# A two-layer graph network kernel: projection biases added in PSUM by VectorE, and the places of five pieces in a written-out order

## The chip, the cores and the metric

The kernel runs on 1 core of one Trainium2 chip. The time is device microseconds from launch to end; a smaller time is better. The engines go by the names of the profile: PE (TensorE, with PEld for its weight loads), DVE (VectorE), ACT (ScalarE), POOL (GpSimd) and SP (SyncE, which here only issues DMAs). PSUM is the memory that PE writes; everything else on the core lies in SBUF.

## The reference

There are 128 graphs (B) of 128 nodes (N) with 64 features (F). About one entry in eight of an adjacency matrix is not zero.

```python
# layer 0: an edge network
h    = maximum(layernorm(x), 0)
mask = (adj > 0)
a    = h @ W1a                                   # W1 = [W1a; W1b], H = 192
e    = relu(a[:, :, None] + (h[:, :, None] - h[:, None]) @ W1b + b1)
hm   = einsum('bjkh,bjk->bjh', e, mask)          # sum over the neighbours k of j
x    = x + hm @ W2 + mask.sum(-1)[..., None] * b2
# layer 1: plain aggregation
h    = maximum(layernorm(x), 0)
x    = x + (adj @ h) @ W.T
```

## The kernel before

Graphs are taken four at a time (G = 4), so there are 32 groups. The inner value of the edge network splits into a part of node j, with the bias, and a part of node k. The kernel doesn't build all 128 x 128 pairs. It gathers each node's neighbours with one-hot matrices: the nodes are cut into four quarters (q), in each quarter a neighbour of j gets a slot (six slots, D = 6), and the few edges that fit no slot go through an extra list of up to 128 edges.

**Jobs.** A group is 24 jobs. A job fills one of three PSUM buffers `g` of two banks with matmuls (tiles S3, k3 and id3) and drains it. Jobs of kind 0 (16 of the 24) are drained by a reduction on DVE into `hm`; jobs of kind 1 (jobs 4, 5, 10, 11, 16, 17, 22, 23, counted from 0) by a Relu on ACT into `T`, which POOL then sums. The same three buffers also take the projection `pp`, twice a group; a second pool of two one-bank buffers takes all smaller products.

**Pieces between the jobs.** After job t the pieces that three tables list for t are issued. `AHEAD` prepares group g+1: `pre_adj` (t = 0; transposes adj into `adjT`, makes `maskT`), `pre_norm`, `pre_hT`, `pre_rank` (3; ranks `qs`), `pre_slots` (3, 4, 6; one-hot `S`, and then twelve DMAs that make S3), `pre_count` (5; `dn`, `ns`, `half`, `nb`), `pre_proj` (7 and 12), `pre_stack` (12; twelve DMAs from `ca` to k3), and `pre_edge_a`, `pre_edge_b`, `pre_place`, `pre_edge_c`, `pre_edge_d` (9 to 23; tiles `et`, `R`, `qj`, `RT`, `S2`). `OWN` makes the edge list's values X (14 and 15, PSUM tile `px`). `BEHIND` ends group g-1: `slot_sum` and `edge_sum` (0, 1; PSUM tile `pe`, result `u`), `edge_sum1`, `post0` (product with W2, PSUM tile `py`, copied by ACT to `ys`), `post1` (transposes back, adds the residual, statistics), `post2` (the second normalization, `h`), `post3` (the aggregation with adjT, `pga`, copied by ACT to `agg`) and `post4` (the last product `po`, the residual and the store of `ot`).

**The projection.** `pre_proj(g, r)` multiplies hT of two graphs with the 448 columns of `wp` into `pp`: 192 columns for node k, 192 for node j and 64 for the output. The bias belongs to the last 256 columns. It is added by PE: a matmul of a tile of ones with `biasp`, whose rows hold the bias split into three bf16 parts (built once in `weights_c`). ACT then copies the first 384 columns as bf16 (`ca`, part 0), makes z and e from pp, DVE subtracts to get `rest`, ACT makes part 1 of ca from it, and POOL part 2. The three parts together carry the fp32 value.

**What sets the order.** PE's instructions stand in the program's order. In the main loop those of the other engines are placed by the framework's scheduler, which also chooses which PSUM buffer a tile gets; within an engine they then run strictly in that order. The framework also adds the waits.

Of the kernel before, what the change touches and what calls it, by code (L numbers as in the profile page):

```python
# [8 lines left out]
F32 = mybir.dt.float32  # L9
BF16 = mybir.dt.bfloat16  # L10
I32 = mybir.dt.int32
AF = mybir.ActivationFunctionType
ALU = mybir.AluOpType
# [137 lines left out]
def kernel(  # L151
# [28 lines left out]
    def mm(*args, **kw):  # L180
        return tc.keep_in_program_order(nc.tensor.matmul(*args, **kw))  # L181
# [21 lines left out]
    vec, act, pool, sp = (Engine(e) for e in (nc.vector, nc.scalar, nc.gpsimd, nc.sync))  # L203

    B, N, F = x.shape
    H = W1.shape[1]
    O = W2.shape[1]
    P = 128
# [19 lines left out]
    with ExitStack() as main:  # L228
        const = main.enter_context(tc.tile_pool(name="const", bufs=1))
        loads = main.enter_context(tc.tile_pool(name="loads", bufs=2))  # L230
        grp = main.enter_context(tc.tile_pool(name="grp", bufs=2))
        one = main.enter_context(tc.tile_pool(name="one", bufs=1))
# [4 lines left out]
        def gtile(name):  # L237
            return ps_g.tile([P, 2, 512], F32, tag="g", name=name)

        def mtile(name):  # L240
            return ps_m.tile([P, 512], F32, tag="m", name=name)
# [7 lines left out]
        w2bd = const.tile([P, 2, O], F32, tag="w2bd", name="w2bd")  # L249
# [3 lines left out]
        ident = const.tile([P, P], F32, tag="ident", name="ident")  # L253
        make_identity(nc, ident)

        id64 = const.tile([P, 4], F32, tag="id64", name="id64")
        vec.tensor_tensor(id64, ident[:, 0:4], ident[:, F : F + 4], ALU.add)
        ones = const.tile([P, P], F32, tag="ones", name="ones")
        pool.memset(ones, 1.0)
        oneb = const.tile([P, P], BF16, tag="oneb", name="oneb")  # L260
# [11 lines left out]
        for q in range(Q):  # L272
            s = slice(q * QN, (q + 1) * QN)
# [43 lines left out]
        bias = const.tile([P, H + O], F32, tag="bias", name="bias")  # L317
        wp = const.tile([P, 2 * H + O], F32, tag="wp", name="wp")
        wab = wp[:, H : 2 * H]
        biasp = const.tile([P, H + O], BF16, tag="biasp", name="biasp")  # L320

        def weight_loads():
            act.dma_start(w2a, W2[0:C0, :])
# [33 lines left out]
            return pc  # L357

        def weights_c(pc):
            left = bias  # L360
            for i in range(3):
                pt = one.tile([P, H + O], BF16, tag=f"bp{i}", name=f"bp{i}")
                vec.tensor_copy(pt, left)

                if i == 0:
                    vec.tensor_scalar(biasp, pt, id64[:, i : i + 1], None, ALU.mult)
                    vec.tensor_copy(wp[:, 2 * H : 2 * H + O], pc[:, 0:O])
                else:
                    vec.scalar_tensor_tensor(
                        biasp, pt, id64[:, i : i + 1], biasp, ALU.mult, ALU.add  # L370
                    )
                if i < 2:
                    nxt = one.tile([P, H + O], F32, tag=f"br{i}", name=f"br{i}")
                    vec.tensor_tensor(nxt, left, pt, ALU.subtract)
                    left = nxt

        def weights_d():
            pl = mtile("pl")
# [5 lines left out]
        def bc(t, n, axis):  # L384
            shape = list(t.shape)
            shape.insert(axis, n)
            return t.unsqueeze(axis).to_broadcast(shape)
# [150 lines left out]
        def pre_proj(g, r):  # L538

            d = groups[g]  # L540
            if r == 0:

                d["ca"] = grp.tile([P, 3, 2, G, H], BF16, tag="ca", name=f"ca{g}")

                d["z"] = grp.tile([P, G, C0], F32, tag="z", name=f"z{g}")
                d["z1"] = grp.tile([P, 2, 2, C1], F32, tag="z1", name=f"z1{g}")
                d["e"] = grp.tile([P, G, O], F32, tag="e", name=f"e{g}", bufs=3)
            pp = gtile(f"pp{g}_{r}")
            for p in range(2):
                s = slice(p * F, (p + 1) * F)  # L550
                mm(
                    pp[:, p, 0 : 2 * H + O], d["hT"][s, r], wp[s, :],
                    start=True, stop=False, skip_group_check=True,
                )
            for p in range(2):
                s = slice(p * F, (p + 1) * F)
                mm(
                    pp[:, p, H : 2 * H + O], oneb[s, :], biasp[s, :],
                    start=False, stop=True, skip_group_check=True,
                )  # L560
            x = pp[:, :, 0 : 2 * H].rearrange("n p (t u) -> n p t u", t=2)
            parts = [
                d["ca"][:, i].rearrange("n t (p r) u -> n r p t u", p=2)[:, r] for i in range(3)
            ]
            act.activation(parts[0], x, AF.Copy)
            rest = tmp.tile([P, 2, 2, H], F32, tag="rest", name=f"rest{g}_{r}")

            def zs():
                for p in range(2):
                    b = 2 * p + r  # L570
                    for to, us, f in (
                        (d["z"][:, b], slice(0, C0), AF.Abs),
                        (d["z1"][:, r, p], slice(C0, H), AF.Relu),
                    ):
                        act.activation(to, x[:, p, 1, us], f, scale=d["ns"][:, b : b + 1])


            def es():
                for p in range(2):
                    b = 2 * p + r  # L580
                    act.activation(
                        d["e"][:, b], pp[:, p, 2 * H : 2 * H + O], AF.Copy,
                        scale=d["dn"][:, 0, b : b + 1],
                    )

            def second():
                act.activation(parts[1], rest, AF.Copy)

            def third(engine):
                for t in range(2):  # L590
                    engine.tensor_tensor(
                        parts[2][:, :, t], rest[:, :, t], parts[1][:, :, t], ALU.subtract
                    )

            def add_x():
                pool.tensor_tensor(d["e"], d["e"], d["x"], ALU.add)

            if g == 0:
                vec.tensor_tensor(rest, x, parts[0], ALU.subtract)
                return zs, es, second, third, add_x  # L600
            zs()
            es()
            vec.tensor_tensor(rest, x, parts[0], ALU.subtract)
            second()
            third(pool)
            if r == 1:
                add_x()
# [143 lines left out]
        def post0(g):  # L751
            d = groups[g]
            py = mtile(f"py{g}")
            d["py"] = py
            for p in range(2):
                s = slice(p * O, (p + 1) * O)
                mm(
                    py[s, 0 : 2 * N], w2h,
                    d["u0"][:, 2 * p : 2 * p + 2].rearrange("h r j -> h (r j)"),
                    start=True, stop=False, skip_group_check=True,  # L760
                )
            w = w2bd.rearrange("h p o -> h (p o)")
            mm(
                py[:, 0 : 2 * N], w, d["u1"].rearrange("h r j -> h (r j)"),
                start=False, stop=True, skip_group_check=True,
            )
            d["ys"] = tmp.tile([P, 2, N], F32, tag="ys", name=f"ys{g}", bufs=1)
            act.activation(
                d["ys"].rearrange("p r j -> p (r j)"), py[:, 0 : 2 * N], AF.Copy
            )  # L770
# [47 lines left out]
        class Job:  # L818
# [71 lines left out]
        AHEAD = {  # L890
            0: (pre_adj,),
            2: (pre_norm, pre_hT,),
            3: (pre_rank, lambda g: pre_slots(g, 0, 2),),
            4: (lambda g: pre_slots(g, 2, 4),),
            5: (pre_count,),
            6: (lambda g: pre_slots(g, 4, D),),
            7: (lambda g: pre_proj(g, 0),),
            9: (pre_edge_a,),
# [10 lines left out]
        BEHIND = {  # L909
            0: (slot_sum,),  # L910
            1: (edge_sum,),
            4: (edge_sum1,),
            8: (post0,),
            10: (post1,),
            15: (post2,),
            16: (post3,),
            19: (post4,),
        }

        ORDER = []  # L920
# [6 lines left out]
        def pieces(table, t, g):  # L927
            if 0 <= g < NG:
                for f in table.get(t, ()):
                    if (f, g) not in early:  # L930
                        f(g)
# [21 lines left out]
        pc = weights_b()  # L953
# [30 lines left out]
        for g in range(NG):  # L984
            if 0 < g < NG - 1:
                load(g + 1)
            order = ORDER0 if g == 0 else ORDERL if g == NG - 1 else ORDER
            for t, args in enumerate(order):
                job = Job(g, *args)
                job.fill()  # L990
                job.drain()
                if g == 0 and t in FIRST:
                    FIRST[t](0)
                pieces(OWN, t, g)
                pieces(BEHIND, t, g - 1)
                pieces(AHEAD, t, g + 1)
        for t in range(T):
            pieces(BEHIND, t, NG - 1)
        om = one.tile([P, 1], F32, tag="om", name="om")
# [34 lines left out]
```

## Time and profile before

| | |
|---|---|
| time, median of 3 runs | 1000.9 us (998.99 to 1002.17) |
| profiled execution | 1005.13 us, span 1003.4 us |
| busy: PE, DVE, POOL, ACT | 94%, 80%, 76%, 70% of the span |
| TensorE clock granted, mean | 0.978 of full |
| distance from one maskT to the next | 29.9 us, mean of 29 in the steady part |
| bias matmuls of pp | 128, 18.1 us busy |
| DMAs for S3 and k3 | 372 and 384, all issued by SP |

A row of the page's groups gives line, engine, operation, tile written <- tiles read, shapes and count; then busy time, the mean of one in ns, and the engine's idle time just before, with what ended most of it. A row of the timeline gives start (us), duration, engine, instruction and count, and in brackets the idle time before it. Rows of equal instructions that follow each other are merged. The next instruction of an engine often starts before the duration shown has run out, so a queue's speed is read from start to start. Almost every line is L198 or L181, since a helper issues the instructions: the tile names tell them apart.

### The profile page before, as it was taken

The numbers are of one execution on the slowest core, as the hardware profiler recorded it, in microseconds if no ns is written. First come the engines' busy times: TensorE is split into PE (matmuls) and PEld (weight loads), VectorE is DVE, ScalarE is ACT, GpSimd is POOL, SyncE is SP. The second block draws the span as 40 slices with busy tenths as digits, with TensorE's granted clock in tenths as the row PEclk, the third lists the DMA queues.
The fourth block names the chain that finished last, engine by engine and source line by source line (L and its number), as shares of the span: only waits on it lengthen the run. The fifth ranks groups of instructions, "written<-read, shape, count | busy, mean of one in ns | idle before, by whom it ended". The sixth has DMA issues, their size and how long they took to land.

```text
span 1003.4 us, 26630 instructions
## 1 busy us (share of the span) xinstructions
PE 947.9 (94%) x9994; PEld 695.8 (69%) x9994; DVE 801.2 (80%) x1769; ACT 706.3 (70%) x1732; POOL 767.5 (76%) x1134
## 2 busy tenths in 40 slices
PE   3899999999999999999999999999999999999996
PEld 2577776677776777777677767677767777777674
DVE  7677888877888878788887787887888887788863
ACT  5557876667877767787677785677787677787652
POOL 3287877787877878877788786778877788787783
PEclk9599999999999999999999999999999999999997
DMA  3626665556766555766555765555766655665520
GB/s 87 134 69 160 153 139 131 127 121 150 157 138 139 129 122 136 164 143 142 126 125 126 159 148 123 124 126 136 164 141 138 134 127 124 157 148 127 111 60 13
DMA packets 88293, 129.89 MB, mean 129 GB/s; under 512 B 47200, under 2 KB 63968, under 8 KB 88160
## 3 DMA queue, kind: packets, MB, share of 16 engines
q1 hardware_dynamic: 87584, 127.98, 56.4%
q8 instruction: 80, 1.31, 0.5%
q14 instruction: 53, 0.43, 0.1%
q10 hardware_dynamic: 576, 0.16, 0.1%
HBM read 13.01 MB, written 4.19 MB: 17 GB/s over the span
## 4 chain that ended last, share of the span: by engine, by line
PE 37%; DVE 23%; ACT 19%; DMA 7%; POOL 6%; issue 4%; SPq 3%; DVEq 0%; POOLq 0%; ACTq 0%
PE g L181 21%; DVE hm L198 7%; DVE S L198 7%; PE pe L181 7%; DMA k<-ca 6%; ACT ca L198 5%; ACT et L198 4%; POOL T L198 4%; SPq L198 3%; ACT h L198 3%; ACT T L198 3%; DVE u L198 3%; POOL ca L198 2%; ACT z L198 2%; PE px L181 2%
## 5 line engine op out<-in xcount | busy, mean ns | idle before, releaser
L198 POOL TENSOR_TENSOR T<-T 128x192 f32<-128x192 f32 (+2 forms) x768 | 545.7, 717 | 124.3 <-ACT T L198 84.4
L198 DVE TENSOR_REDUCE hm<-g 128x64 f32<-128x768 f32 x512 | 473.4, 950 | 117.0 <-PE g L181 113.2
L181 PEld LDWEIGHTS <-k 96*128 96x128 bf16 (+1 forms) x6144 | 412.8, 104 | 213.9 <-issue 87.0
L181 PE MATMUL g<-S,k 96*128 96x384 bf16 (+1 forms) x2048 | 392.5, 333 | 34.9 <-DMA k<-ca 18.5
L181 PE MATMUL g<-id,k 96*128 96x192 bf16 (+1 forms) x4096 | 383.9, 248 | 0.0
L198 ACT ACTIVATE T<-g 128x768 f32<-128x768 f32 x256 | 210.2, 823 | 51.7 <-PE g L181 45.7
L198 POOL TENSOR_TENSOR ca<-rest,ca 128x384 bf16<-128x384 f32 x126 | 113.9, 924 | 85.3 <-ACT ca L198 83.6
L198 ACT ACTIVATE ca<-pp 128x768 bf16<-128x768 f32 x64 | 51.4, 804 | 63.7 <-PE pp L181 63.7
L198 DVE TENSOR_TENSOR S<-qs,rks 128x1024 bf16<-128x1024 bf16 x93 | 86.8, 934 | 0.0
L198 ACT ACTIVATE hT<-ph 128x256 f32<-128x256 f32 x32 | 12.3, 384 | 89.4 <-PE ph L184 89.4
L181 PE MATMUL pe<-RT,X 128*64 128x128 f32 (+1 forms) x512 | 71.3, 282 | 0.0
L181 PE MATMUL pp<-wp,hT 64*128 64x448 f32 x256 | 68.5, 613 | 0.0
L198 ACT ACTIVATE z<-pp,ns 128x128 f32<-128x128 f32 (+1 forms) x256 | 66.0, 348 | 0.0
L198 DVE TENSOR_TENSOR rest<-pp,ca 128x768 f32<-128x768 f32 x64 | 60.7, 949 | 3.0 <-ACT ca L198 2.8
L198 ACT ACTIVATE ca<-rest 128x768 bf16<-128x768 f32 x64 | 55.2, 862 | 9.3 <-DVE rest L198 9.2
L181 PEld LDWEIGHTS pe<-RT,X 128*64 128x64 f32 (+1 forms) x512 | 53.4, 166 | 5.3 <-issue 5.3
L198 ACT ACTIVATE et<-et,half 128x128 f32<-128x128 f32 x128 | 56.8, 449 | 0.0
L181 PE MATMUL px<-ca,S 128*128 128x192 bf16 x384 | 52.7, 246 | 0.0
L181 PE MATMUL px<-ca,R 128*128 128x192 bf16 x384 | 52.6, 246 | 0.0
L198 ACT ACTIVATE h<-x,mrb,rsb 128x64 f32<-128x64 f32 x128 | 51.6, 479 | 0.8 <-DVE mrb L198 0.8
L181 PE MATMUL pe<-ident,z 128*128 128x128 f32 x192 | 49.9, 287 | 0.0
L198 ACT ACTIVATE h<-x,mra,rsa 128x64 f32<-128x64 f32 x128 | 48.7, 432 | 1.1 <-DVE mra L198 1.1
(128 smaller groups left out, 1203.9 us busy)
## 6 DMA issues: line engine op xcount, KB each, us to landing
S<-S SPq DMA_DIRECT2D x372, 192.0 KB, 4.0
k<-ca SPq DMA_DIRECT2D x384, 96.0 KB, 2.2
adj<-in_adj_dram SPq DMA_DIRECT2D x32, 256.0 KB, 3.1
x<-in_x_dram SPq DMA_DIRECT2D x32, 128.0 KB, 2.7
out_dram<-ot SPq DMA_DIRECT2D x32, 128.0 KB, 2.2
w<-in_L_gnn_W_dram SPq DMA_DIRECT2D x2, 96.0 KB, 4.4
bias<-in_L_gnn_b_dram ACTq DMA_DIRECT2D x1, 96.0 KB, 3.8
w2a<-in_L_gnn_W_dram ACTq DMA_DIRECT2D x1, 32.0 KB, 2.1
```

Source lines behind the costliest of these rows:

```text
L181: return tc.keep_in_program_order(nc.tensor.matmul(*args, **kw))
L198: ins = f(*args, **kw)
```

## The change

Two things are changed. First, the bias of the projection: the two matmuls with `biasp` are gone, and so are `biasp`, `id64` and the eight DVE instructions in `weights_c` that built it (with the one for id64, nine in all). In their place one DVE `tensor_tensor` adds the fp32 bias in place to 256 columns of both halves of `pp` in PSUM, before ACT and DVE read it. Second, the places of BEHIND's pieces: edge_sum1 from 4 to 3, post0 from 8 to 9, post1 from 10 to 11, post3 from 16 to 21, post4 from 19 to 23; at t = 3, 9 and 21 the piece of AHEAD now comes before that of BEHIND. In post0 the product with u1 comes before those with u0.

```diff
         def weights_c(pc):
-            left = bias
-            for i in range(3):
...
+            vec.tensor_copy(wp[:, 2 * H : 2 * H + O], pc[:, 0:O])
...
                 mm(
                     pp[:, p, 0 : 2 * H + O], d["hT"][s, r], wp[s, :],
-                    start=True, stop=False, skip_group_check=True,
-                )
-            for p in range(2):
-                s = slice(p * F, (p + 1) * F)
-                mm(
-                    pp[:, p, H : 2 * H + O], oneb[s, :], biasp[s, :],
-                    start=False, stop=True, skip_group_check=True,
-                )
+                    start=True, stop=True, skip_group_check=True,
+                )
+            biased = pp[:, :, H : 2 * H + O]
+            vec.tensor_tensor(biased, biased, bc(bias, 2, 1), ALU.add)
...
         BEHIND = {
             0: (slot_sum,),
             1: (edge_sum,),
-            4: (edge_sum1,),
-            8: (post0,),
-            10: (post1,),
+            3: (edge_sum1,),
+            9: (post0,),
+            11: (post1,),
             15: (post2,),
-            16: (post3,),
-            19: (post4,),
+            21: (post3,),
+            23: (post4,),
         }
...
                 pieces(OWN, t, g)
+                if t in (3, 9, 21):
+                    pieces(AHEAD, t, g + 1)
                 pieces(BEHIND, t, g - 1)
-                pieces(AHEAD, t, g + 1)
+                if t not in (3, 9, 21):
+                    pieces(AHEAD, t, g + 1)
```

More of the change, by code (lines that the diff above doesn't have):

```diff
@@ L254 @@
         make_identity(nc, ident)
-        id64 = const.tile([P, 4], F32, tag="id64", name="id64")
-        vec.tensor_tensor(id64, ident[:, 0:4], ident[:, F : F + 4], ALU.add)
         ones = const.tile([P, P], F32, tag="ones", name="ones")
@@ L319 @@
         wab = wp[:, H : 2 * H]
-        biasp = const.tile([P, H + O], BF16, tag="biasp", name="biasp")
         def weight_loads():
@@ L359, in weights_c @@
         def weights_c(pc):
-            left = bias
-            for i in range(3):
[L362 to L370, printed above, removed]
-                    )
[L372 to L375, printed above, removed]
+            vec.tensor_copy(wp[:, 2 * H : 2 * H + O], pc[:, 0:O])
         def weights_d():
@@ L754, in post0 @@
             d["py"] = py
+            w = w2bd.rearrange("h p o -> h (p o)")
+            mm(
+                py[:, 0 : 2 * N], w, d["u1"].rearrange("h r j -> h (r j)"),
+                start=True, stop=False, skip_group_check=True,
+            )
             for p in range(2):
@@ L759, in post0 @@
                     d["u0"][:, 2 * p : 2 * p + 2].rearrange("h r j -> h (r j)"),
-                    start=True, stop=False, skip_group_check=True,
+                    start=False, stop=True, skip_group_check=True,
                 )
[L762 to L766, printed above, removed]
             d["ys"] = tmp.tile([P, 2, N], F32, tag="ys", name=f"ys{g}", bufs=1)
```

## The prediction

> **What bounds the kernel now.** I read the busy shares first, then who waits for whom, then one group of the steady part (391 to 425 us) engine by engine in order of time.
>
> ```profile
> PE 947.9 (94%) x9994; PEld 695.8 (69%) x9994; DVE 801.2 (80%) x1769; ACT 706.3 (70%) x1732; POOL 767.5 (76%) x1134
> ```
>
> ```profile
> PE g L181 <- DMA k<-ca: 18.5, 22, 7.2
> PE g L181 <- DVE hm L198: 15.2, 31, 0.6
> ```
>
> TensorE (PE) is hardly ever idle, and the waits in front of it are small: 0.5 us a group for VectorE (DVE), and some tenths, where a group begins, for the last DMA of k3. So PE has about 1 us a group to spare, and each other engine is free for 20 to 30% of the time. An average doesn't say where that time lies; the order of time does. A group repeats every 29.9 us (the 29 distances between maskT instructions, from 67.9 to 935.4 us). The stretch that the change touches, DVE first, then ScalarE (ACT), then PE:
>
> ```profile
> 395.02 0.68 DVE L198 TENSOR_SCALAR maskT<-adjT 128x512 bf16<-128x512 f32 x1 [1.13 <-PE pe L181]
> ...
> 401.37 2.80 DVE L198 TENSOR_REDUCE hm<-g 128x64 f32<-128x768 f32 x3
> 404.09 0.95 DVE L198 TENSOR_TENSOR rest<-pp,ca 128x768 f32<-128x768 f32 x1
> ...
> 401.85 0.81 ACT L198 ACTIVATE ca<-pp 128x768 bf16<-128x768 f32 x1 [1.87 <-PE pp L181]
> 402.56 1.03 ACT L198 ACTIVATE z<-pp,ns 128x128 f32<-128x128 f32 x4
> 403.45 0.55 ACT L198 ACTIVATE e<-pp,dn 128x64 f32<-128x64 f32 x2
> 404.43 0.38 ACT L198 ACTIVATE ys<-py 128x256 f32<-128x256 f32 x1 [0.43 <-PE py L181]
> 405.07 0.84 ACT L198 ACTIVATE ca<-rest 128x768 bf16<-128x768 f32 x1 [0.26 <-DVE rest L198]
> 405.95 0.81 ACT L198 ACTIVATE T<-g 128x768 f32<-128x768 f32 x1
> ...
> 401.54 0.28 PE L181 MATMUL pp<-biasp,oneb 64*128 64x256 bf16 x2
> 402.36 0.48 PE L181 MATMUL g<-S,k 96*128 96x384 bf16 x2 [0.55 <-DVE hm L198]
> ...
> 407.69 1.02 PE L181 MATMUL pp<-wp,hT 64*128 64x448 f32 x4
> ```
>
> DVE works from maskT (395.02) to 407.6 with hardly a gap. When the first projection pp is done (401.82), DVE still owes three reductions, but ACT is idle and reads pp at once, because PE itself has put the bias in. That start, 401.85, is what the change gives away.
>
> **What goes.** The two bias matmuls of a projection: 0.28 us a pair, two pairs a group. The first pair gains nothing: the next matmul (402.36) waits for DVE's hm in any case, and its 0.55 us of idle time become 0.82. The second pair gains up to 0.27 us. If PE were the bound and both pairs counted, the gain would be 62 x 0.27 = 17 us; I count 0.27 a group on PE. In the prologue, eight DVE instructions for biasp (8.76 to 12.13 us) go, but the next wait there, for qs (ACT, until 12.41), leaves 0.6 us of that; the second of the new adds comes behind the first rest, so that the second rest moves from 18.01 to about 18.8. Sum: +0.8 us.
>
> The Trainium skill ("Perfetto Trace Analysis", Identifying the Most-Contended Engine) calls matmul busy time no good measure of how close PE is to its limit. The row above, 94%, taken by itself would promise the 17 us; by the page it promises nothing.
>
> **What comes.** One DVE add of 128x512 (fp32, PSUM and SBUF in, PSUM out) for each projection. No row writes PSUM from DVE. The nearest reads PSUM and SBUF at the same size:
>
> ```profile
> L198 DVE TENSOR_TENSOR u<-hs,pe 128x512 f32<-128x512 f32 x32 | 21.6, 676 | 2.7 <-POOL hs L198 1.6 <-POOL T L198 1.1
> L198 DVE TENSOR_TENSOR x<-pty,e 128x256 f32<-128x256 f32 x32 | 13.6, 425 | 4.5 <-PE pty L184 2.0
> ```
>
> I take 0.67 us (next instruction after 0.60); the ends are 0.42 (half the size) and 0.95 (rest, 768 columns). A gain is excluded: an instruction is added to a queue that has no gap there. 64 x 0.67 = 43 us of DVE. What counts is its place. The built program has it on DVE behind hm of jobs 6 and 7, and ca, z, e and everything behind them in ACT's queue wait for it.
>
> The skill ("PSUM — Partial Sum Buffer", PSUM bank collisions) says that no two engines may be in one PSUM bank at once, reads included. Here too rest begins at 404.09, right behind the last e (404.00), though ca, which it reads, was done at 402.66; without that rule rest could come 1.3 us earlier, but as ACT is busy by then, the sum below would stay.
>
> **One group worked through** with the built order and waits, each instruction by its start-to-start time in these rows (us of the window above):
> - DVE up to nb, 401.37: as before. hm6 and hm7 take 0.87 each, the add runs 403.10 to 403.77. ca starts at 403.82 instead of 401.85: **1.97 late**.
> - ACT from there: ca 0.69, four z 0.89, two e 0.39, ys 0.26, three et 0.88 (they now stand ahead), ca second part 0.73 (its rest runs 405.95 to 406.9, just in time), one et 0.29, then T of job 10 at 407.98. It ends at 408.79; before, at 406.76.
> - PE: the second pp takes the PSUM buffer of job 10 and waits for that T. PE gets there at 407.79 (job 9 at 403.24 behind hm7, pv and py 1.2, jobs 10 and 11 at 0.78, pty 0.37, job 12 at 0.76), so it **stalls 1.05 us**, until 408.84.
> - ACT goes on without a gap: T of job 11, sdb, three et, three h until 411.42. Only then the second ca (its add ended at 411.0), 2.4 later than before; z, e, X, h, et, sda until 414.66; second part of ca until 415.5, X, T of jobs 16 and 17 at 415.82 and 416.51. PE's jobs 19 and 20 take their buffers: 0.55 us of stall. Then R, four h, and qj until 419.75: 15.9 us of ACT work from 403.82 in one piece.
> - PE: the aggregation pga, now behind job 21, takes the buffer that qj frees: 419.80, 0.4 us of stall. From there to the next edge_sum only PE's own work: pga 0.44, jobs 22 and 23 1.51, po 0.47, pgq 0.33, job 0 0.65, pt 0.44, job 1 0.71. edge_sum begins at 424.35, where the group before began it at 392.73: **31.6 us, 1.7 more than the mean** of 29.9. Of ca's 1.97 us, 0.7 of ACT's gaps behind it are eaten, the rest is passed on; the k3 wait at the group's start goes.
>
> **What moves at no cost:** edge_sum1 one job earlier (0.86 us of PE; T of job 4 comes 0.9 later, and ACT has 0.74 of gap before T of job 5); py's matmuls in another order (both inputs are there long before); post0 and post1 one job later (their place is in the sum). po delays pgq by 0.47 us; S2 on DVE is then done at 423.5, before edge_sum wants its buffer (424.35). Without that cover it would cost 0.5 a group. On SyncE's queue the store of ot stands behind the twelve k3 DMAs, whose last was issued at 420.04; ot is now ready at 422.8, so the store and the two loads behind it go out 1.9 us later; the loads are two groups early, and the next S3 DMAs come 8 us later. The k3 DMAs: their first now waits for the second ca (412.2 instead of 411.46), the second four for its second part (415.5); the last lands near 422.3, before job 1 wants it (423.6). No instruction of POOL changes place; its ca third ends at 417.3, and k3's last four want it at 418.1.
>
> **Sum.** POOL being slightly less in DVE's way at S (0.60 instead of 0.92 to 1.08 us in such moments) may give 0.1 back: 1.6 x 30 groups = 48, and the prologue 1: +49 us. The profiled execution took 1005.1 us (span 1003.4, 1.7 around it), 4.2 over the median of 1000.9; so 1054 there, and 1050 for the median. The add's bounds (-0.25, +0.28 a group) are -8 and +8 us.
>
> **Rivals.**
> - *PE is the bound and the add hides.* Price: 62 pairs x 0.27 = 17 us less, 984. For it: 94%. Against it: T of job 10 had 0.93 us in hand (406.76 to 407.69) and gets 2.0 later. It decides if the add ran before hm6 and hm7, which the built order excludes, or if ca came less than 0.9 late.
> - *Part of the stalls is made up.* Stalls in a row overlap, and a later PE finds its buffers free: only the stall at the second pp stays, 1.05 less the 0.27: 0.8 x 30 = 24 and 1, 1026. For it: after job 20 the margins are some tenths. Against it: ACT's queue has no gap until qj.
> - *The k3 chain becomes late.* If the DMAs kept the slow issue that some show before (0.9 instead of 0.64 us), the eight behind the second part would end 2 us later, land at 424.4 and hold job 1 by 0.8 a group: 24 more, 1074. It decides from 1.3 us of lateness on. Against it: they no longer queue right behind the S3 DMAs.
>
> **How the numbers follow.** The solid ACT queue (1.2 to 2.1 a group, 1037 to 1065): 0.68. Part made up (down to 1010): 0.17. k3 late: 0.08. Hidden: 0.05, and 0.02 for a draw. Likeliest 1050; the range 1022 to 1066 leaves out the hidden case, most of the late one and the lower part of the middle one. A change of 0.3% (3 us) is about what a measurement of this kernel can tell from none: faster 0.05, same 0.02, slower 0.93.
>
> **What would show it.** Right: maskT every 31.5 us; ca<-pp waiting for DVE's pp; PE idle before pp<-wp for ACT's T, some 1 us each time; ACT without a gap from the first ca to qj; no wait for k. Wrong: pp<-wp starting without a wait; a bias add far from 0.67 us; maskT below 30.5 or above 32.5; PE waiting for k<-ca in most groups.

## The result, and the profile after

The changed kernel took 1048.94 us (median of 6 runs, 1046.55 to 1049.13) against 997.93 us (994.83 to 1002.17, 6 runs) of the kernel before on the same chip: a ratio of 1.0502 (95% interval 1.0474 to 1.0531), 51 us slower. The ratios here and below are those on record; they are not the quotients of the two medians. The forecast was 1050 us in a range of 1022 to 1066. The profiled execution of the changed kernel took 1046.55 us (span 1044.8); it had been put at 1054.

The first line of the page, busy time and share of the span by engine:

```profile
PE 934.6 (89%) x9866; PEld 700.1 (67%) x9866; DVE 843.5 (81%) x1824; ACT 695.2 (67%) x1732; POOL 759.6 (73%) x1134
```

PE lost 128 instructions and 13.3 us of busy time, DVE gained 42.3. PE's share of the span fell from 94% to 89% while the span grew. The time is in waits, and the waits of PE and ACT say where (total us, times, longest):

```profile
PE pp L181 <- ACT T L198: 31.7, 30, 1.1
PE g L181 <- DVE hm L198: 22.9, 32, 0.9
PE g L181 <- ACT T L198: 13.7, 31, 0.6
PE g L181 <- DMA k<-ca: 8.8, 1, 8.8
PE pga L181 <- ACT qj L198: 7.7, 29, 0.3
ACT ca L198 <- DVE pp L198: 63.2, 18, 3.9
```

Before, PE's list began with k<-ca (22 times) and hm (31 times, 15.2 us). The wait for k is left once, 26 us into the program. Three waits for ACT are new, each in nearly every group: the second projection pp for a T, a job's buffer g for a T, the aggregation pga for qj. The last row is the cause that the prediction named: ca cannot start before DVE's add.

The order of one steady group, from the same stretch as the one shown of before (maskT at 409.43, the next at 440.92). DVE:

```profile
409.43 0.46 DVE L198 TENSOR_SCALAR maskT<-adjT 128x512 bf16<-128x512 f32 x1 [1.14 <-PE pe L181]
...
415.49 1.80 DVE L198 TENSOR_REDUCE hm<-g 128x64 f32<-128x768 f32 x2
417.21 0.68 DVE L198 TENSOR_TENSOR pp<-pp,bias 128x512 f32<-128x512 f32 x1
417.81 1.80 DVE L198 TENSOR_REDUCE hm<-g 128x64 f32<-128x768 f32 x2
...
420.11 0.96 DVE L198 TENSOR_TENSOR rest<-pp,ca 128x768 f32<-128x768 f32 x1 [0.35 <-ACT e L198]
...
440.92 0.46 DVE L198 TENSOR_SCALAR maskT<-adjT 128x512 bf16<-128x512 f32 x1 [1.14 <-PE pe L181]
```

The add stands behind hm of jobs 6 and 7. PE had ended pp at 415.76; the add ended at 417.89, 2.1 us later, of which only 0.68 is its own length. ACT then, in the same group:

```profile
417.93 0.81 ACT L198 ACTIVATE ca<-pp 128x768 bf16<-128x768 f32 x1 [3.78 <-DMA S<-S]
...
419.92 0.43 ACT L198 ACTIVATE ys<-py 128x256 f32<-128x256 f32 x1
420.18 1.03 ACT L198 ACTIVATE et<-iov,mid 128x128 f32<-128x128 f32 x3
421.10 0.85 ACT L198 ACTIVATE ca<-rest 128x768 bf16<-128x768 f32 x1
421.85 0.39 ACT L198 ACTIVATE et<-iov,mid 128x128 f32<-128x128 f32 x1
422.14 1.50 ACT L198 ACTIVATE T<-g 128x768 f32<-128x768 f32 x2
```

(The first row's wait is put down to a DMA, "S<-S"; the add's end, 0.04 us before ca's start, is what 18 other such waits in the list above are put down to, and the nearer cause.) Between ys and the T of job 10 stand four et and the second part of ca. And PE, every row of the group with an idle time over 0.2 us:

```profile
416.48 0.48 PE L181 MATMUL g<-S,k 96*128 96x384 bf16 x2 [0.72 <-DVE hm L198]
422.99 1.02 PE L181 MATMUL pp<-wp,hT 64*128 64x448 f32 x4 [1.06 <-ACT T L198]
431.10 0.48 PE L181 MATMUL g<-S,k 96*128 96x384 bf16 x2 [0.44 <-ACT T L198]
434.20 0.66 PE L181 MATMUL pga<-adjT,h 128*64 128x128 f32 x8 [0.26 <-ACT qj L198]
```

The distance between two maskT is 31.51 us (mean of 29 groups) against 29.92. This "period" is the measure in what follows; it is steadier than the time of a run. 29 groups at 1.60 us are 46.4 us; the median moved by 51 and the two profiled executions by 41.4. The difference between these last two numbers is no property of the change: see the last section.

### The profile page after: what moved, and what is told of

It reads as the page before. It is cut to its first block, busy times and chain, and to the rows that moved or that the text cites. A ratio compares the mean times of both kernels' runs of the same rounds, so it can differ in the third digit from the quotient of the medians.

```text
span 1044.8 us, 26521 instructions
## 1 busy us (share of the span) xinstructions
PE 934.6 (89%) x9866; PEld 700.1 (67%) x9866; DVE 843.5 (81%) x1824; ACT 695.2 (67%) x1732; POOL 759.6 (73%) x1134
## 4 chain that ended last, share of the span: by engine, by line
ACT 40%; DVE 24%; PE 23%; issue 7%; DMA 4%; DVEq 0%; POOL 0%; POOLq 0%; ACTq 0%
PE g L181 10%; DVE S L198 8%; ACT T L198 8%; ACT h L198 8%; PE pe L181 6%; DVE hm L198 6%; ACT z L198 5%; ACT ca L198 5%; ACT et L198 4%; DMA S<-S 4%; DVE u L198 3%; ACT X L198 3%; PE pga L181 2%; PE po L181 2%; DVE mrb L198 2%
## 5 line engine op out<-in xcount | busy, mean ns | idle before, releaser
L198 POOL TENSOR_TENSOR T<-T 128x192 f32<-128x192 f32 (+2 forms) x768 | 538.1, 707 | 125.9 <-ACT T L198 85.9
L181 PEld LDWEIGHTS <-k 96*128 96x128 bf16 (+1 forms) x6144 | 424.2, 104 | 228.7 <-issue 119.7
L181 PE MATMUL g<-S,k 96*128 96x384 bf16 (+1 forms) x2048 | 380.6, 328 | 52.0 <-DVE hm L198 22.9
L198 ACT ACTIVATE T<-g 128x768 f32<-128x768 f32 x256 | 195.0, 821 | 50.0 <-PE g L181 50.0
L198 ACT ACTIVATE hT<-ph 128x256 f32<-128x256 f32 x32 | 12.3, 383 | 90.6 <-PE ph L184 90.6
L198 DVE TENSOR_TENSOR ot<-po,x 128x256 f32<-128x256 f32 x32 | 13.6, 424 | 68.0 <-PE po L181 68.0
L181 PEld LDWEIGHTS pp<-wp,hT 64*128 64x128 f32 x256 | 19.8, 189 | 44.3 <-ACT T L198 38.5
```

The source lines that it names most:

```text
L198: ins = f(*args, **kw)
```

## The experiments

For each kernel the trace gives, besides the period, the idle times in front of PE's matmuls, averaged over 28 steady groups. Nearly all stand in the same few places. In the table a dash is a place with less than 0.06 us; "job n" is the first matmul of that job, and the columns go in the order of time. The ends of matmuls are modelled and small waits are left out, so a row doesn't sum exactly to the period; it shows which wait is there. The times are medians taken on several chips, on which the kernel before had medians of 997.9 to 1003.9 us; a ratio given below always compares with the kernel before on the same chip.

| kernel | time, us | period | job 8 (hm) | pty (ys) | second pp (T of job 10) | job 13 (hm) | jobs 19, 20 (T) | pga |
|---|---|---|---|---|---|---|---|---|
| before | 1000.9 | 29.92 | 0.49 | - | - | - | - | - |
| no bias, old places | 1000.7 | 30.01 | 0.58 | - | - | 0.10 | - | - |
| late end only | 999.5 | 29.82 | 0.45 | - | - | - | - | - |
| second add only, old places | 1016.3 | 30.37 | 0.54 | - | - | 0.10 | - | 0.57 (h) |
| both adds, old places | 1036.6 | 31.05 | 0.66 | 0.43 | - | 0.10 | - | 0.81 (h) |
| both adds, late end | 1018.0 | 30.45 | 0.53 | 0.50 | - | 0.10 | 0.54 | - |
| five places alone | 1012.4 | 30.39 | 0.74 | - | - | 0.56 | 0.36 | - |
| five places, no bias | 1004.0 | 30.07 | 0.74 | - | - | 0.67 | 0.23 | - |
| five places, adds of 4 columns | 1016.4 | 30.37 | 0.85 | - | - | 0.67 | 0.25 | - |
| five places, second add only | 1016.2 | 30.33 | 0.62 | - | - | 0.67 | 0.66 | - |
| five places, first add only | 1061.5 | 31.97 | 0.86 | - | 1.05 | - | 1.15 | - |
| changed kernel | 1048.9 | 31.51 | 0.73 | - | 1.06 | - | 0.44 | 0.26 (qj) |
| changed, pre_edge_a later | 1011.2 | 30.26 | 0.74 | - | - | - | 0.95 | - |
| changed, et's second step on DVE | 1049.1 | 31.49 | 0.72 | - | 1.06 | - | 0.49 | - |

Not in the columns: the kernel before, the one without bias and the one with the late end wait for k<-ca at the start of many of their groups (22, 22 and 14 times, 18.5, 19.9 and 14.4 us in all, of which 6.4 to 7.2 are one wait in the first groups), and a few rows have one more wait of 0.1 to 0.4 us.

### The two halves

**The adds alone** (the old tables; post0 with u0 first, as before):

```diff
+            biased = pp[:, :, H : 2 * H + O]
+            vec.tensor_tensor(biased, biased, bc(bias, 2, 1), ALU.add)
-            for p in range(2):
...
```

> Only the bias moves to the DVE add; the pieces keep their old places. Theory A (the prediction's: the add's place behind two reductions starts ACT's queue 2 us late, and ACT then works without a gap until qj): the whole loss or most of it, 1030 to 1050 us. Theory B (the new places make the loss, because the scheduler then puts work ahead of T of job 10 and ahead of qj in ACT's queue): under 1005 us. Worked through with this kernel's built order, where T of job 10 stands ahead of ca's second part, so that the second pp does not wait for it, and where three of the four h stand behind RT: 0.6 us a group remain, 1016 us; then A and B each hold a part.

Measured: 1036.55 us, ratio 1.0364 (1.0305 to 1.0422). That lies in the range of theory A, but the way there is another, and the sum worked through for this build (1016) was 20 us short. PE's waits:

```profile
PE pga L181 <- ACT h L198: 27.4, 32, 2.7
PE g L181 <- DVE hm L198: 20.4, 31, 0.7
PE pty L184 <- ACT ys L198: 13.5, 31, 0.5
```

The late first ca does not reach PE at the second pp here, for in this build the T of job 10 stands right behind ys. It reaches PE through ys (at pty) and then through h, since at its old place, behind job 16, the aggregation pga comes before ACT has made h.

**The five places alone** (the bias stays on PE):

> Only the places (with post0's order of products); the bias stays on PE. Theory A: no change beyond 6 us either way, 991 to 1004 us, since ca still starts as soon as pp is done. Theory B: most of the loss, 1030 us or more. Worked through: pga behind job 21 waits for qj, but ACT reaches qj early; 998 us.

Measured: 1012.41 us, ratio 1.0122 (1.0066 to 1.0177). That is more than theory A allowed and far less than theory B asked for. The prediction had moved these pieces "at no cost". They cost 0.47 us a group.

```profile
PE g L181 <- DVE hm L198: 38.8, 60, 0.8
PE g L181 <- ACT T L198: 11.6, 30, 1.3
```

PE now waits for hm twice a group instead of once. The second place is job 13, whose buffer is that of a job drained by hm, and on DVE an instruction that waits stands ahead of that hm:

```profile
411.42 0.42 DVE L198 TENSOR_TENSOR x<-pty,e 128x256 f32<-128x256 f32 x1 [0.88 <-PE pty L184]
411.88 0.61 DVE L198 BATCH_NORM_STATS2 stb<-x 128x6 f32<-128x64 f32 x4
412.40 0.36 DVE L198 BATCH_NORM_AGGREGATE mvb<-stb 128x2 f32<-128x6 f32 x4
412.68 0.93 DVE L198 TENSOR_REDUCE hm<-g 128x64 f32<-128x768 f32 x1
```

With post1 one job later, its transpose pty comes one job later, x waits 0.88 us for it with DVE otherwise free, and the statistics and hm queue behind x. In the kernel before, x has no such wait:

```profile
406.26 0.42 DVE L198 TENSOR_TENSOR x<-pty,e 128x256 f32<-128x256 f32 x1
```

The PE row that pays:

```profile
413.66 0.48 PE L181 MATMUL g<-S,k 96*128 96x384 bf16 x2 [0.56 <-DVE hm L198]
```

### What the bias matmuls were worth

**The changed kernel without the adds** (no bias at all, which leaves the biases out of the result; new places):

> The changed kernel without the DVE add; the projection's biases are left out altogether. Theory A: the loss is gone, 988 to 999 us, a few us under before, because the bias matmuls are gone too and only the second pair of a group was worth anything (0.27 us x 31 = 8 us at most). Theory B: the loss stays, 1030 us or more. If PE were the bound and both pairs counted, 17 us under before: 981 us.

Measured: 1003.95 us, ratio 1.0032 (1.0001 to 1.0063), period 30.07. The loss is gone, as theory A had it, but the few us under the kernel before that it expected did not come. Against the five places alone the two pairs are worth 0.32 us a group, 8 us.

**The kernel before without the bias matmuls** (biases left out of the result; old places):

```diff
-                    start=True, stop=False, skip_group_check=True,
+                    start=True, stop=True, skip_group_check=True,
-            for p in range(2):
+            for p in range(0):
```

> The kernel before without any bias on the projection (no bias matmuls, no add in their place; the biases are left out of the result), its places as they were. It bounds what moving the bias off PE can bring at best. Theory A (small waits of PE for DVE's hm swallow part of the 0.54 us a group of bias matmuls; with the new places taking them out was worth 0.32 a group): 0.3 x 31 = 10 us less, about 990, period 29.6. Rival (PE is the bound, both pairs count): 0.54 x 31 = 17 less, 984 or below, period 29.4. Rival (the wait for k's DMAs or for hm takes all of it): 998, period 29.9.

Measured: 1000.7 us (12 runs) against 998.98 (23 runs), ratio 0.9997 (0.9972 to 1.0023). At the old places the bias matmuls cost nothing that this measurement can tell (a gain of 0.3% at most); the rival that put it at 998 with period 29.9 is the one that holds. The second projection of one group:

```profile
406.27 1.02 PE L181 MATMUL pp<-wp,hT 64*128 64x448 f32 x4
407.39 0.48 PE L181 MATMUL g<-S,k 96*128 96x384 bf16 x2
```

maskT of this group is at 393.59, so the job behind pp starts 13.80 us into the group. In the kernel before it started at 408.81 with maskT at 395.02: 13.79. It starts when an hm is done (the table's job 13). In the kernel before, that hm and PE's rows around it are:

```profile
407.79 0.96 DVE L198 TENSOR_REDUCE hm<-g 128x64 f32<-128x768 f32 x1 [0.20 <-PE g L181]
```

```profile
408.54 0.28 PE L181 MATMUL pp<-biasp,oneb 64*128 64x256 bf16 x2
408.81 0.49 PE L181 MATMUL g<-S,k 96*128 96x384 bf16 x2
```

This hm ends at 408.75, 1.06 us after pp's first matmul (407.69). The four matmuls of pp take 0.85 of that from start to start and the bias pair the rest, so that the pair lay under a wait that could not be seen. So moving the bias off PE could gain nothing that shows at these places, whatever it cost elsewhere.

### The add: its length, its place, and which of the two

**Adds of 4 columns instead of 256** (the rest of the biases left out of the result):

```diff
-            biased = pp[:, :, H : 2 * H + O]
-            vec.tensor_tensor(biased, biased, bc(bias, 2, 1), ALU.add)
+            biased = pp[:, :, H : H + 4]
+            vec.tensor_tensor(biased, biased, bc(bias[:, 0:4], 2, 1), ALU.add)
```

> The changed kernel with the DVE add over 4 of the 256 columns of each half (the other columns get no bias): the wait for DVE's queue stays, the add takes 0.15 instead of 0.68 us. Theory A (the place counts): ca starts 1.4 to 1.5 us late instead of 2.0; the built order has T of job 10 ahead of ca's second part, so no stall at the second pp; 1000 to 1012 us, above the kernel without an add. Theory C (the 43 us of DVE work itself are the loss): the same as without an add, within 3 us.

Measured: 1016.35 us, ratio 1.0167 (1.0105 to 1.0228). This fits neither theory cleanly. The add took 158 ns instead of 676, yet the first ca came 8.30 us into the group instead of 8.51: the place behind two reductions makes it late, not its length. But 32 us of the loss went. This build has another order on ACT: T of job 10 is right behind ys again, and the second pp doesn't wait. The run changes the length and the order together; that the order can do it without the length is shown by pre_edge_a two jobs later, below, where the adds are whole and the period is 30.26 against 30.37 here.

**Only one of the two adds**, the other projection's bias left on PE (new places; with r == 1 in the line shown for the second only):

```diff
+            if r == 0:
                 biased = pp[:, :, H : 2 * H + O]
                 vec.tensor_tensor(biased, biased, bc(bias, 2, 1), ALU.add)
```

> New places; the DVE add for the first projection of a group only, the second keeps its bias matmuls. By the working of the prediction the first add starts the lateness (ca 2 us late, T of job 10 behind ca's second part, the second pp stalled by 1.05 us), and the second runs while ACT is behind anyway: 31.0 to 31.4 us a group (new places alone: 30.4; changed kernel: 31.5), 1030 to 1045 us. Rival (each add costs its own length): half of the way, 30.95 us, 1031 us, and the same for the second one alone.

> New places; the DVE add for the second projection only. T of job 10 stands ahead of ca's second part again, and pp finds its buffer free; the second ca comes about 1.3 us late behind hm of job 12, with gaps of ACT to eat it: 30.4 to 30.8 us a group, 1012 to 1024 us. Rival (each add costs its own length): 30.95 us, 1031 us.

Measured: first only 1061.54 us, ratio 1.0616 (1.0591 to 1.064), slower than both adds and outside what either theory expected. Second only 1016.23 us, ratio 1.0145 (1.011 to 1.018), the same period as the places alone (30.33 and 30.39). So the second add costs nothing at the new places, and the loss comes with the first one. Why one add is worse than two is in ACT's order once more. In the first-only kernel:

```profile
435.17 0.78 ACT L198 ACTIVATE R<-et,ones 128x512 bf16<-128x512 f32 x1
435.78 1.57 ACT L198 ACTIVATE T<-g 128x768 f32<-128x768 f32 x2
```

R stands ahead of the two T here, behind them in the changed kernel, and PE's job 19 waits 1.15 us for T instead of 0.44. With the wait of 0.26 at pga gone, that is 0.45 more, and the period is 0.46 longer. Only the order was read, not changed by itself.

**The second add in the kernel before** (first bias on PE, old places):

> The kernel before with only the second projection's bias added by DVE, the first one's still by PE, and the places as before. In the new places the second add alone cost nothing and brought nothing (period 30.32 against 30.39). Theory A (the second add has cover, since ACT has work of its own at that point, and PE saves one pair of 0.27): 992 to 1000, period 29.65 to 29.9. Rival (ACT's h comes behind z, e and X of the late second ca, and the aggregation pga at its old place waits for h as it did with both adds): 1005 to 1020, period 30.2 or more, PE waiting at pga for ACT h in most groups.

Measured: 1016.25 us, ratio 1.0164 (1.0122 to 1.0206). The rival holds: what is free at the new places is not free at the old ones.

```profile
PE pga L181 <- ACT h L198: 19.9, 31, 2.7
```

The second ca is 0.7 us later (14.59 instead of 13.90 into the group), the four h stand behind its z, e and X, and pga at job 16 waits for them.

### ACT's queue

**pre_edge_a two jobs later** in the changed kernel; no other line of the program is different:

```diff
-            9: (pre_edge_a,),
+            11: (pre_edge_a,),
```

> The changed kernel with one piece moved: pre_edge_a (four et on ACT) at 11 instead of 9. Both adds keep their length and ca its lateness of 2 us; the built order has T of jobs 10 and 11 ahead of ca's second part and of et, and three of the four h behind RT. Theory A (what is late is ACT's queue, in the order it is given): the queue reaches qj 1.3 us earlier, 30.2 to 30.6 us a group, 1006 to 1020 us. Theory C (the length of the adds on DVE): no change beyond 5 us, 1043 us or more.

Measured: 1011.19 us, ratio 1.0095 (1.0065 to 1.0126), as theory A had it. One line of a table takes back 38 of the 51 us. ACT of one group (maskT at 398.26):

```profile
406.73 0.81 ACT L198 ACTIVATE ca<-pp 128x768 bf16<-128x768 f32 x1 [3.76 <-DMA S<-S]
...
408.73 0.43 ACT L198 ACTIVATE ys<-py 128x256 f32<-128x256 f32 x1
408.99 1.57 ACT L198 ACTIVATE T<-g 128x768 f32<-128x768 f32 x2
410.37 0.92 ACT L198 ACTIVATE ca<-rest 128x768 bf16<-128x768 f32 x1
```

The first ca is as late as in the changed kernel (8.47 us after maskT in this group, 8.50 there), and the adds are as long. But both T now stand ahead of the second part of ca and of the four et, and on PE:

```profile
410.65 1.02 PE L181 MATMUL pp<-wp,hT 64*128 64x448 f32 x4
```

no wait. The period falls by 1.25 us, more than the 1.06 of that stall, though job 19 waits 0.95 instead of 0.44 and job 11 a new 0.19 for T; the 0.26 at pga are gone. These idle times make up a part of the 1.25 only, and the rest stands in no wait that the profile shows. The second ca also comes 1.5 us earlier in the group here (14.93 instead of 16.41), so the run turns ACT's order from T of job 10 on, and not that T alone.

**The second step of et on DVE**, which takes about 1.2 us a group from ACT's queue behind the second pp:

```diff
-                act.activation(
-                    d["et"][:, b, :], d["et"][:, b, :], AF.Relu, bias=d["half"][:, b : b + 1]
+                vec.tensor_scalar(
+                    d["et"][:, b, :], d["et"][:, b, :], d["half"][:, b : b + 1], 0.0,
+                    ALU.add, ALU.max,
```

> The changed kernel with the second step of et (four Relu with a bias, 4 x 0.29 us) on DVE instead of ACT. T of job 10 stays behind ca's second part, so the second pp waits as long as before. Theory A (ACT's queue without a gap until qj sets the group): 0.8 to 1.2 us a group less, 1013 to 1026 us. If the visible wait of the second pp is the loss: 1043 to 1050 us. Theory C (DVE's work): slower, as DVE gets 0.5 us a group more, 1055 us or more.

Measured: 1049.12 us, ratio 1.0482 (1.0457 to 1.0506), period 31.49: unchanged, in the range that was put for the wait of the second pp as the loss. ACT now has gaps before qj:

```profile
427.79 1.10 ACT L198 ACTIVATE h<-x,mrb,rsb 128x64 f32<-128x64 f32 x3 [0.17 <-DVE mrb L198]
436.39 0.60 ACT L198 ACTIVATE qj<-pj 128x512 bf16<-128x512 f32 x1 [0.35 <-PE pj L181]
```

and PE's wait at pga is gone, but the group is no shorter. The run doesn't settle it alone, since the same work on DVE gave PE a new wait of 0.40 us for hm at job 16, about as much as it took away. It shows that ACT's queue being solid up to qj is not needed for 31.5 us.

### The late places, one half at a time

**Only the end moved** in the kernel before (post3 to 21 behind AHEAD's piece, post4 to 23):

> The kernel before with only the aggregation and the last product moved (post3 at 21 behind the piece of AHEAD, post4 at 23); edge_sum1, post0 and post1 stay at 4, 8 and 10, and the bias stays on PE. All five places together cost 12 us (1012.4). Theory A (the loss comes from edge_sum1, post0 and post1, which leave PE without work between jobs 8 and 13, where it now waits 0.6 us a group more for DVE's hm): about 999, period 29.9. Rival (it comes from the late end: agg, po and pgq stand right before the next group's edge_sum): about 1012, period 30.4.

Measured: 999.49 us (12 runs), ratio 0.9988 (0.996 to 1.0017). The late aggregation and last product are free: here the prediction was right. By subtraction the cost of the five places comes with edge_sum1, post0 and post1, or with what else went along with them in that run: the other order of py's products, and AHEAD's piece ahead of BEHIND's at t = 3 and 9. None of these was changed by itself.

**Both adds with the late end only**:

```diff
-            3: (edge_sum1,),
-            9: (post0,),
-            11: (post1,),
+            4: (edge_sum1,),
+            8: (post0,),
+            10: (post1,),
```

> The changed kernel with edge_sum1, post0 and post1 back at 4, 8 and 10 (behind them the pieces of AHEAD as before); both adds stay, and the aggregation and last product stay at 21 and 23. Seen from the run with the adds alone (1036.6), only the aggregation and the last product move. Theory A (what the late ca costs is decided by single waits of PE: at the old places pty waits 0.43 for ACT's ys and pga 0.81 for ACT's h, and at job 21 pga no longer meets h; T of job 10 stays right behind ys in ACT's queue, so the second pp does not stall): period 30.3 to 30.7, about 1017; up to 1028 if job 19 waits for T as in the run with pre_edge_a later. Rival (the late ca is passed on whatever the places): 1036 and more, period 31.05. Rival (only the five places together with the add make the loss, and without the three early moves nothing is left of it): about 1001.

Measured: 1018.0 us, ratio 1.0151 (1.012 to 1.0183), period 30.45.

```profile
PE g L181 <- ACT T L198: 17.5, 31, 1.2
PE g L181 <- DVE hm L198: 17.0, 32, 0.7
PE pty L184 <- ACT ys L198: 15.6, 31, 0.5
```

Against both adds at the old places, the wait at pga is gone and the one at pty stays, as the first theory had it. (Two things differ between those two kernels, not one as was expected: besides the late end, post0 has the product with u1 first here.) This is the best way found to have both adds with pre_edge_a at its place, and still 1.5% slower. None of the kernels run was faster than the kernel before by what the measurement can tell.

## Why the prediction was right, and where its reasons were not

The sum was right: 1.6 us a group was predicted, 1.60 measured, and +0.8 us in the prologue stands against 1.0 (the second maskT at 27.73 instead of 26.76). That the two agree so closely is in part luck: the three stalls that the sum has on PE add up to 2.0 us and measured 1.76, and a cost that the sum left out happens not to show in this build. Step by step:

- **The add.** 0.67 us from the row of u, measured 0.676. Its place behind hm of jobs 6 and 7: as built. ca 1.97 us late in the worked group; the mean is 1.70 (6.81 to 8.51 after maskT), and 0.19 of the difference is that nb comes earlier: maskT takes 0.38 us from start to start instead of 0.51, and the three S instructions 0.07 less together, for which the sum had allowed 0.1.
- **T of job 10 and the second pp.** Predicted 1.05 us of stall, measured 1.06, each time. This was the step that mattered most: in the run with pre_edge_a later, where T stands ahead of et, the stall is gone and the time is 1011 us, though more of ACT's order differs there than this T.
- **What follows.** Predicted 0.55 at jobs 19 and 20 and 0.4 at pga, measured 0.44 and 0.26. The wait for k went as predicted.
- **What the bias matmuls bring.** 0.27 us a group for the second pair was the bound taken into the sum. At the old places it is zero as far as can be measured: job 13 starts when an hm ends, pair or no pair. At the new places both pairs bring 0.32. The Trainium skill's "Perfetto Trace Analysis" (Identifying the Most-Contended Engine), which calls matmul busy time no good measure of PE's limit, is not contradicted: 12.3 us of busy time less on PE (947.9 to 935.6) gave no time. The page's reason is that pipelined matmuls look smaller in a trace; here the pair lay under a wait for hm.
- **"What moves at no cost"** is the step that failed. The five places cost 0.47 us a group (1012.4 us) and the late end alone nothing (999.5), which leaves the cost with post0 and post1 one job later and edge_sum1 one earlier, or with py's order that went along. I had followed PE and ACT, and for edge_sum1 the T behind it, but not DVE's queue: x, which waits for pty, stands ahead of an hm that a job needs. In the changed kernel that wait doesn't show, since PE comes to job 13 later anyway, held by the second pp. So the error did not appear in the sum.
- **"Of ca's 1.97 us, 0.7 of ACT's gaps are eaten, the rest is passed on"** falls as an explanation. Kernels whose first ca is equally late (8.5 to 8.8 us after maskT) have periods of 30.26, 30.45, 31.05 and 31.51. Lateness has no fixed price; it is paid where a matmul meets a late T, ys or h, and that went with the order on ACT and with the places. The condition put against the second rival, that ACT's queue has no gap until qj, was true of the build, but the loss doesn't need it: with gaps in the queue the period was the same, though that run put a wait for hm in the place of the one at pga.
- **The rivals.** "Hidden" asked for ca less than 0.9 late, and fell with that. "Part made up" asked that only the second pp's stall stay; all three stayed. "k3 late" fell: k is waited for once. Its last DMA is issued 25.13 us after maskT, 0.7 later than before, in a group that became 1.6 longer.
- **The skill's rule on PSUM banks** ("PSUM — Partial Sum Buffer", PSUM bank collisions), which the prediction set beside rest starting right behind e: after the change rest does so again (420.11, with e ending at 420.08). But the program itself makes rest wait for e (61 of the 64 times, by DVE's waits), so these rows don't show the rule, and no run here tests it. And in the group before, rest could not have come 1.3 us earlier in DVE's order: it stands behind three hm, which end at 404.17, and follows them without idle time.

What stays open: why the framework's scheduler puts T of job 10 behind four et and the second part of ca in three of these builds and right behind ys in the others. The order is read from the built programs; no run here changes the scheduler's rule.

## What to carry to other kernels

Before taking work off the busiest engine, run the kernel with that work left out: here that run says that the matmuls cost nothing at their places, so that moving them could not gain. Where an instruction is added between a producer and its first reader, look at its place in its engine's queue rather than at its length, and then at what the engine of the reader has in front of the next buffer that is needed. Moving a piece by one job moves every instruction behind it on each engine, and one that waits (x for pty) holds up its whole queue behind it; and a change in a table can turn the order elsewhere, so compare the built orders before explaining a difference by the edit itself.

## What was not expected of the chip

Single executions of one kernel differ by several microseconds (the kernel before: 994.77 to 1007.35 in all runs), and the first two groups are one place where that arises. In the profiled execution of before, the third maskT came at 67.86 us, in that of the changed kernel at 62.53, though its prologue is 1.0 us longer. The granted clock differs in the same stretch: from 20 to 60 us, in steps of 10, TensorE was granted 0.51, 0.50, 0.67 and 0.79 of full speed in the one, and 0.50, 0.65, 1.00 and 1.00 in the other. What made it come up later in the one is not shown. The 5.3 us between the two third maskT account for the difference between the 46.4 us that the periods alone make and the 41.4 by which the two profiled executions differ. Over the traces of all fourteen kernels the third maskT lies between 61.8 and 70.2 us. So the period is the better measure: two traces are best compared after the clock has come up.

The add in place in PSUM took as long as the same add from PSUM to SBUF (676 ns for 512 fp32 elements of 128 partitions, against 675 of u<-hs,pe in the same trace). An add of 8 elements took 158 ns (adds of 4 columns), so most of the 676 goes with the number of elements.
